# Keeping the sums of fc's weight blocks in DRAM: one transformer block with attention over a context, on one Trainium2 core

## The chip, the cores and the metric

The kernel runs on one core of a Trainium2 chip. Its time is the device time of one execution in microseconds; a measurement is the median of several executions, and shorter is better. The engines of the core have names in the profile: PE (TensorE, matrix products), DVE (VectorE), ACT (ScalarE), POOL (GpSimd) and SP (SyncE, which here only issues DMA transfers). The program gives each engine its own list of instructions, issued in the order in which the kernel's code calls them, and they wait for each other by semaphores.

## The reference, cut to what matters

Everything is float32. There are B = 4 batches; a batch has L = 512 rows of D = 512 numbers, and the hidden layer of the MLP has 2048 columns.

```python
def layer_norm(x, w, b): ...
x   = layer_norm(hidden_states, ln1_w, ln1_b)
q   = x @ q_w + q_b                       # 16 heads of 32
k   = encoder_hidden_states @ k_w + k_b
v   = encoder_hidden_states @ v_w + v_b
out = softmax(q @ k.T / sqrt(32), masked) @ v
hidden = out @ cproj_w + cproj_b + hidden_states
y   = layer_norm(hidden, ln2_w, ln2_b)
y   = gelu(y @ fc_w + fc_b)               # fc:   512 -> 2048
y   = y @ proj_w + proj_b                 # proj: 2048 -> 512
return hidden + y
```

## The kernel before

**Two parts.** The first part runs the attention of all batches as 32 blocks (16 groups of four heads, two halves each). The order is written out by hand: `put(p, ...)` names the other work that is filled into block p, and the program is issued in that order on every engine. Most of the MLP of batch 0 and half of that of batch 1 are such fillings. The second part, `last_mlps`, does the rest of batch 1's MLP (pairs 4 to 7 of fc and proj) and all of the MLPs of batches 2 and 3, one after the other.

**fc by seven products.** fc works on pairs of 128-column blocks of its weight; a batch has 8 pairs. `fc_seven` computes one pair by Winograd's form of Strassen's method: weight and input are cut into 2 by 2 blocks, and seven block products replace eight. Each of the seven is two matmuls, which stand as four rows in the trace (L518), so a pair is 28 rows. The products want sums of blocks: of the input (`y_sums`, once a batch, written to `ys` and into `yT`), and of the weight pair (`a_sums`, four subtractions or additions of 128 x 256 numbers: s1, s2, s3 and s4). These and all other sums stand in the trace at L472 (`add`) and L469 (`sub`). The products come in the order a11, a12, s2, s3, s1, s4, a22; the fourth takes the input sum t3 (written into `yT`), the seventh t4 (in `ys`). DVE then adds the products together into `ga` (or `gt`), and ACT applies gelu (L539).

**Where the weight sums are made.** For batch 0 and the first four pairs of batch 1, `fc_sums` makes them on POOL into `wsum` (s3 overwrites a block of the raw weight). In the second part `load_wa(c)` (L598, SP queue) loads the raw pair c into one of two buffers inside the tile `gt`, and `sum_wa(c)` makes its sums on DVE. `fc_pair(c)` issues `sum_wa(c + 1)` on DVE ahead of the additions of its own pair c.

**proj by seven products, some split once more.** `project` multiplies the gelu output `ga` (cut into g11, g12, g21, g22) with proj's weight (b11 to b22) by the same seven products, q1 to q7. `g_sums` (two pairs at a time) and `p_sums` make the sums. A plain product is 16 matmuls, 32 rows at L701 or L719. In batches 2 and 3 the products 3, 6, 7 and 5 are cut once more by `forty_nine`, which makes seven small products of four 128-wide matmuls (56 rows at L664); in batch 3 product 2 is, too. Each such split wants `x_sums` of its left side (three operations on DVE and one on POOL) and `w_sums` of its right side (four on DVE, from the list `to_split`, taken off by `split(n)`).

**Other work around it.** POOL copies a part of each attention block's transposed probabilities (`pT`, L335) while SP moves the rest by DMA (L340); the `av` products (L357) of block p are issued two blocks later and wait for both. `load_hid` loads the rows of a batch to which proj's result is added (SP, L413) and adds proj's bias on POOL (`add_row`, L368); for batch 2 it stands after pair 5 of batch 1. `load_xn` (L406), the loads of proj's weight (L461, L817) and the stores (L714, L786) share the SP queue. `stat2` (L127) computes layer-norm statistics on DVE.

Of the kernel before, what the change touches and what calls it, by code (L numbers as in the profile page):

```python
# [12 lines left out]
F32 = mybir.dt.float32  # L13
# [37 lines left out]
def xattn_block(ctx: ExitStack, tc: tile.TileContext, x, encT, mask, q_w, k_w, v_w, c_w, fc_w, p_w, vecs, rows, out):  # L51
# [422 lines left out]
    def a_sums(a11, a12, a21, a22, s1, s2, s3, s4, engine=None):  # L474
        add(engine or nc.vector, s1, a21, a22)
        sub(s3, a11, a21, engine)
        sub(s2, s1, a11, engine)
        sub(s4, a12, s2, engine)
# [18 lines left out]
    def acc_half(name):  # L497
        return acc_tile(name).rearrange("p (i l) -> p i l", i=2)
# [7 lines left out]
    def fc_seven(b, c, g, a, s, half, q=None):  # L506
# [35 lines left out]
        if q is None:  # L542
            gelus()

    fc_pairs = [(0, c) for c in range(NP)] + [(SPLIT, c) for c in range(FIRST * FQ // 2)]

    def raw_pair(b, c):
# [2 lines left out]
    def fc_sums():  # L550

        while count[3] < len(fc_pairs) and count[3] < count[4] + 2:
            b, c = fc_pairs[count[3]]
            if ("fcw", b, 2 * c + 1) not in S:
                return
            x, y = raw_pair(b, c)
            s = wsum[:, count[3] % 2]
            a_sums(x[:, :2], x[:, 2:], y[:, :2], y[:, 2:], s[:, 0], s[:, 1], y[:, :2], s[:, 2], nc.gpsimd)
            S["ws", b, c] = s[:, 0], s[:, 1], y[:, :2], s[:, 2]
            count[3] += 1  # L560

# [32 lines left out]
    ws = [gt[:, i * 2048 + 1024 : i * 2048 + 2048].rearrange("p (i k f) -> p i k f", i=4, k=2) for i in range(2)]  # L594

    def load_wa(c):
        for i in range(2):
            nc.sync.dma_start(out=wa[c % 2][:, i], in_=fc_w[:, 2 * c + i, :, :])  # L598

    def sum_wa(c):  # L600
        a = wa[c % 2]
        a_sums(a[:, 0, :2], a[:, 0, 2:], a[:, 1, :2], a[:, 1, 2:], *(ws[c % 2][:, i] for i in range(4)))

    def p_sums(c):

# [4 lines left out]
    def last_mlps():  # L610
# [73 lines left out]
            a11, a12, a21, a22 = (ga[:, c, k, j * HL : (j + 1) * HL] for j in range(2) for k in range(2))  # L684
            a_sums(a11, a12, a21, a22, gs[:, 0, c], gs[:, 1, c], a21, gs[:, 2, c])

        def fc_pair(b, c, sums):
            sums()
            fc_seven(b, c, ga[:, c], [wa[c % 2][:, i] for i in range(2)],
                     [ws[c % 2][:, i] for i in range(4)], half_tile)  # L690

        def project(b, pairs, sums, turns, middle):
            g11, g12, g21, g22 = (ga[:, :, k, j * HL : (j + 1) * HL] for j in range(2) for k in range(2))
            b11, b12, b21, b22 = (pb[:, :, k, j * HL : (j + 1) * HL] for k in range(2) for j in range(2))
            t1, t2, t3, t4 = pt[:, 0], pt[:, 1], b12, pt[:, 2]
            s1, s2, s3, s4 = gs[:, 0], gs[:, 1], g21, gs[:, 2]

            def product(o, a, w, ts_=range(2)):
                for t in ts_:
                    for c in pairs:  # L700
                        nc.tensor.matmul(  # L701
                            o[:, t], a[:, c, ts(t, P)], w[:, c], start=(c == pairs[0]), stop=(c == pairs[-1])
                        )

            def hid(i, j, t):
                return S["hid", b, 2 * i + t][:, j * HL : (j + 1) * HL]

            def join(engine, i, j, src):
                for t in range(2):
                    add(engine, hid(i, j, t), src[:, t], hid(i, j, t))  # L710

            def store(i, j):
                for t in range(2):
                    nc.sync.dma_start(out=out[b, ts(2 * i + t, P), j * HL : (j + 1) * HL], in_=hid(i, j, t))  # L714

            q1 = acc_half(f"q1p_{b}")
            steps = [(t, c) for c_ in (pairs[:-1], pairs[-1:]) for t in range(2) for c in c_]
            for n, (t, c) in enumerate(steps):
                nc.tensor.matmul(  # L719
                    q1[:, t], g11[:, c, ts(t, P)], b11[:, c],  # L720
                    start=n == 0, stop=c == pairs[-1], skip_group_check=t > 0,
                )
            nc.scalar.copy(p1p, q1)
            sums()
            if b > SPLIT:
                if b == B - 1:
                    x_sums(g12, x_more)
                else:
                    split(4)
                x_sums(s4, g11)  # L730
                if b == B - 1:
                    forty_nine(b, "2", u3p, g12, b21, x_more, 4)
                    q2 = u3p
                else:
                    q2 = acc_half(f"q2p_{b}")
                    product(q2, g12, b21)
                turns()
                join(nc.gpsimd, 0, 0, p1p)
                join(nc.gpsimd if b == B - 1 else nc.vector, 0, 0, q2)
                store(0, 0)  # L740
                x_sums(s2, g12)
                if b < B - 1:
                    split(4)
                forty_nine(b, "3", u3p, s4, b22, g11, 0)
                join(nc.gpsimd, 0, 1, u3p)
                x_sums(s3, s4)
                forty_nine(b, "6", u2p, s2, t2, g12, 1)
                add(nc.vector, u2p, u2p, p1p)
                x_sums(s1, s2)
                forty_nine(b, "7", u3p, s3, t3, s4, 2)  # L750
                add(nc.vector, u3p, u3p, u2p)
                for i, j, src in ((0, 1, u2p), (1, 0, u3p), (1, 1, u3p)):
                    join(nc.gpsimd, i, j, src)
                forty_nine(b, "5", p1p, s1, t1, s2, 3)
                join(nc.vector, 0, 1, p1p)
                join(nc.vector, 1, 1, p1p)
            else:
                q2 = acc_half(f"q2p_{b}")
# [12 lines left out]
                product(q7, s3, t3)  # L771
                add(nc.vector, u3p, q7, u2p)
                for i, j, src in ((0, 1, u2p), (1, 0, u3p), (1, 1, u3p)):
                    join(nc.gpsimd, i, j, src)
                q5 = half_tile(f"q5p_{b}")
                product(q5, s1, t1)
                join(nc.vector, 0, 1, q5)
                join(nc.vector, 1, 1, q5)
            store(0, 1)
            store(1, 1)  # L780
            middle()
            q4 = half_tile(f"q4p_{b}"), acc_half(f"q4p_{b}")
            for t in range(2):
                product(q4[t], g22, t4, (t,))
                add(nc.vector, hid(1, 0, t), q4[t][:, t], hid(1, 0, t))
                nc.sync.dma_start(out=out[b, ts(2 + t, P), :HL], in_=hid(1, 0, t))  # L786

        half = FIRST * FQ // 2
        to_split = (
            w_sums(2, pb[:, :, 0, HL:]) + w_sums(3, pt[:, 0])  # L790
            + w_sums(0, pb[:, :, 1, HL:]) + w_sums(1, pt[:, 1]) + w_sums(4, pb[:, :, 1, :HL])
        )
        splits = {(B - 2, 1): 2, (B - 2, 3): 3, (B - 2, 5): 3, (B - 1, 1): 2, (B - 1, 3): 2}

        def split(n):
            for _ in range(n):
                to_split.pop(0)()

        for b, pairs, new in (
            (SPLIT, range(half, NP), range(half)), (SPLIT + 1, range(NP), ()), (SPLIT + 2, range(NP), ())  # L800
        ):
            for c in pairs:

                def sums(b=b, c=c):
                    if c + 1 < NP:
                        sum_wa(c + 1)
                    split(splits.get((b, c), 0))

                fc_pair(b, c, sums)
                if c + 2 < NP:  # L810
                    load_wa(c + 2)
                elif b + 1 < B:
                    load_wa(c + 2 - NP)
                if new:
                    n = (c - half + 2) % half
# [2 lines left out]
                if c % 2 == 0 and c != pairs[0]:  # L818
                    g_sums(c - 2)

                if (b, c) in ((SPLIT, half + 1), (B - 1, half - 1)):
                    load_hid(max(b, SPLIT + 1), range(NT))
                if b == B - 3 and c < NP - 1:
                    stat2(B - 1, c - pairs[0])
                if b == B - 2:
# [7 lines left out]
            def sums(b=b, new=new):  # L833
                for c in new[::2]:
                    p_sums(c)

            def turns(b=b):
                if b + 1 < B:
# [4 lines left out]
            def middle(b=b):  # L843
                if b + 1 < B:
                    y_sums(b + 1)
                    sum_wa(0)

            project(b, pairs, sums, turns, middle)

# [120 lines left out]
    def put(p, *work, before=()):  # L970

        work = [item for part in work for item in part]
        ahead[p] = list(before)
        fills[p] = work
# [18 lines left out]
    put(9, c[:1], do(lambda: attend(3, 1)), x2[:2], c[1:2], x2[2:], stat(0, 0), c[2:3], stat(0, 1),  # L993
        c[3:], stat(0, 2), x3, stat(0, 3), rs(0))
    k, q, v = A(8)
    put(10, [k], norm(0, 0, 1), [v], norm(0, 2, 3), do(fc_sums), [q], t2, do(lambda: y_sums(0)))
    k, q, v = A(9)
    put(11, [k, v], some(2), pb_(0))

    x1, x2, x3, x4 = inputs(3)  # L1000
    put(12, [q], some(2), x1)
# [53 lines left out]
    run(mlp + norm(2, 2, 3))  # L1055
    p_sums(first_c)
    load_wa(first_c + 1)
    sum_wa(first_c)
    c = C(B - 1)
    run(c[:2])  # L1060
    p_sums(first_c + 2)
# [47 lines left out]
```

## Time and profile before

| what | value |
|---|---|
| median of 3 runs | 771.92 us (770.52 to 774.0) |
| the profiled execution | 771.6 us |
| its span, first to last instruction | 769.8 us |
| granted TensorE clock in it | 1.000 |
| PE busy | 762.7 us (99%) |
| DVE busy | 616.4 us (80%) |
| ACT busy | 336.8 us (44%) |
| POOL busy | 298.1 us (39%) |
| DMA moved | 119.37 MB, 155 GB/s on average |

The span is 1.8 us shorter than the execution's time: that much lies before its first and after its last instruction. Rows of the timeline give a start, a duration, the engine, the line of the kernel, the operation, what it writes and reads, how many instructions were merged, and in brackets how long the engine had been idle before and who released it. Rows of the chain give a start, a duration, the engine and the line: it is the sequence of work that ended last, followed back from the end. A pair of fc in the second part is 28 rows of L518; batch 1 has its pairs 4 to 7 from about 523 us on, batch 2 its eight pairs from about 577 us, batch 3 from about 673 us.

### The profile page before, as it was taken

Reading aid. Unit: us, or ns where it says so; the run is one execution under the profiler, and the core shown is the slowest. Engines: PE = TensorE matmul, PEld = TensorE weight load, DVE = VectorE, ACT = ScalarE, POOL = GpSimd, SP = SyncE. Lnnn points to the kernel's source line nnn. Section 1 sums busy time; section 2 is a strip of 40 time slices with the busy share of each in tenths; the row PEclk is TensorE's granted clock in tenths of the full one; section 3 lists DMA queues with packets and bytes.
Section 4 is the critical chain, followed back from the end, with each engine's and each line's share of the span. In section 5 each row is a group of like instructions: output and inputs, shape, how many; then the busy total and the mean of one; then the engine's idle time right before and its main releaser. Section 6 shows DMA issues by size and latency. Waiting matters only on the chain.

```text
span 769.8 us, 12991 instructions
## 1 busy us (share of the span) xinstructions
PE 762.7 (99%) x4450; PEld 519.1 (67%) x4450; DVE 616.4 (80%) x1263; ACT 336.8 (44%) x760; POOL 298.1 (39%) x311
## 2 busy tenths in 40 slices
PE   9999999999999999999999999999899999999998
PEld 6656555566654745565554566447788889988897
DVE  3889899887899757877887989776858997679872
ACT  2676766564775454638753567401102221022200
POOL 1525447378454363235565544330320004202052
PEclk9999999999999999999999999999999999999999
DMA  8978689466766666565756777773523310024001
GB/s 327 319 224 225 179 208 259 101 158 180 215 173 161 182 188 169 139 184 136 176 134 179 206 223 180 171 241 129 172 96 85 93 55 14 31 85 147 0 16 41
DMA packets 54817, 119.37 MB, mean 155 GB/s; under 512 B 10416, under 2 KB 13616, under 8 KB 54624
## 3 DMA queue, kind: packets, MB, share of 16 engines
q1 hardware_dynamic: 53712, 115.71, 54.1%
q0 software_dynamic: 896, 2.82, 1.2%
q8 instruction: 35, 0.57, 0.3%
q14 instruction: 30, 0.25, 0.1%
q10 hardware_dynamic: 144, 0.02, 0.0%
HBM read 58.22 MB, written 6.82 MB: 84 GB/s over the span
## 4 chain that ended last, share of the span: by engine, by line
PE 97%; DVE 2%; DMA 0%; issue 0%; ACT 0%; POOL 0%; DVEq 0%; POOLq 0%
PE q L518 24%; PE accp L574 11%; PE sc L260 8%; PE av L357 8%; PE accv L240 8%; PE acck L217 7%; PE accq L229 7%; PE r L664 7%; PE accc L397 7%; PE q4p L701 2%; PE q1p L719 2%; PE tp L158 2%; PE q2p L701 1%; DVE ga L472 1%; PE warm L901 1%; PE q3p L701 0%
## 5 line engine op out<-in xcount | busy, mean ns | idle before, releaser
L270 ACT ACTIVATE ptt<-ptt,mn 128x512 f32<-128x512 f32 x256 | 181.6, 711 | 149.8 <-DVE mn L266 149.8
L266 DVE CUSTOM_DVE_ANT_0 ptt<-sc,mb 128x512 f32<-128x512 f32 x256 | 160.5, 682 | 18.7 <-PE sc L260 18.6
L278 DVE STREAM_TRANSPOSE tb<-ptt 128x1024 f32<-128x1024 f32 x128 | 153.5, 1218 | 0.3 <-ACT ptt L270 0.2
L335 POOL COPY pT<-tb 32x1088 f32<-32x1088 f32 x96 | 104.5, 1088 | 39.9 <-DVE oT L362 14.6
L574 PE MATMUL accp<-pbt,gt 128*128 128x512 f32 x192 | 84.9, 596 | 0.0
L518 PE MATMUL q<-yT,gt 128*128 128x256 f32 x320 | 78.9, 379 | 0.0
L539 ACT ACTIVATE ga<-ga,vec 128x512 f32<-128x512 f32 x40 | 26.7, 714 | 98.5 <-DVE ga L472 98.5
L574 PEld LDWEIGHTS accp<-pbt,gt 128*128 128x128 f32 x192 | 35.8, 190 | 45.9 <-issue 39.4
L518 PEld LDWEIGHTS q<-yT,gt 128*128 128x128 f32 x320 | 60.8, 190 | 8.7 <-issue 0.5
L260 PE MATMUL sc<-pbt 32*128 32x512 f32 x512 | 65.3, 614 | 0.0
L240 PEld LDWEIGHTS accv<-ptt,xe 128*128 128x128 f32 x512 | 59.1, 192 | 7.4 <-DVE mn L266 4.7
L518 PE MATMUL q<-ys,gt 128*128 128x256 f32 x240 | 61.7, 379 | 0.0
L240 PE MATMUL accv<-ptt,xe 128*128 128x128 f32 x512 | 60.0, 276 | 0.0
L217 PE MATMUL acck<-xe,ptt 128*128 128x512 f32 x128 | 59.1, 604 | 0.0
L229 PE MATMUL accq<-xe,ptt 128*128 128x512 f32 (+1 forms) x136 | 58.3, 573 | 0.0
L397 PE MATMUL accc<-wc,oT 128*128 128x512 f32 x128 | 56.4, 596 | 0.0
L518 PEld LDWEIGHTS q<-ys,gt 128*128 128x128 f32 x240 | 45.5, 190 | 6.6 <-DVE gt L469 0.4
L270 ACT ACTIVATION_READ_ACCUMULATOR ptt<-ptt,mn 128x1 f32 x256 | 47.8, 187 | 0.0
L252 POOL TENSOR_TENSOR v<-v,row 128x512 f32<-128x512 f32 x16 | 20.5, 1282 | 67.6 <-ACT v L245 67.4
L357 PE MATMUL av<-pT,v 128*32 128x256 f32 x768 | 46.4, 382 | 0.0
L229 PEld LDWEIGHTS accq<-xe,ptt 128*128 128x128 f32 x136 | 25.0, 190 | 30.8 <-issue 23.2
L397 PEld LDWEIGHTS accc<-wc,oT 128*128 128x128 f32 x128 | 23.8, 190 | 30.8 <-issue 27.4
(182 smaller groups left out, 1186.3 us busy)
## 6 DMA issues: line engine op xcount, KB each, us to landing
pT<-tb SPq DMA_DIRECT2D x288, 136.0 KB, 2.4
pbt<-p_w_dram SPq DMA_DIRECT2D x40, 256.0 KB, 3.1
gt<-fc_w_dram SPq DMA_DIRECT2D x40, 256.0 KB, 2.7
gt<-tb SPq DMA_DIRECT2D x48, 136.0 KB, 2.4
xe<-tb SPq DMA_DIRECT2D x48, 136.0 KB, 2.4
pbt<-fc_w_dram SPq DMA_DIRECT2D x24, 256.0 KB, 3.7
ptt<-k_w_dram SPq DMA_DIRECT2D x16, 256.0 KB, 3.6
xe<-encT_dram SPq DMA_DIRECT2D x16, 256.0 KB, 5.0
```

Source lines behind the costliest of these rows:

```text
L217: nc.tensor.matmul(acc, S["wk", w][:, d, :], eT[:, d, :], start=(d == 0), stop=(d == ND - 1))
L229: nc.tensor.matmul(acc, S["wq", w][:, d, :], xT[:, d, c], start=(d == 0), stop=(d == ND - 1))
L240: nc.tensor.matmul(acc[:, ts(t, P)], eT[:, d, ts(t, P)], S["wv", w][:, d, :], start=(d == 0), stop=(d == ND - 1),)
L260: nc.tensor.matmul(S["sc", w, qt][h], qT[r, ts(qt, P)], kT[r, :], start=True, stop=True)
L266: nc.vector.tensor_tensor_reduce(out=s, in0=S["sc", w, qt][h], in1=S["mb", w // NG], scale=1.0, scalar=FMAX, op0=ALU.add, op1=ALU.min, acc ...
L270: nc.scalar.activation(s, s, AF.Exp, bias=mn, scale=-1.0, accum_out=S["sums", w][:, qt, h : h + 1])
L278: nc.vector.transpose(tv[:, qt % 2, 2 * k : 2 * k + 2], S["ps", w, qt, k])
L335: nc.gpsimd.tensor_copy(pT[ts(i, HD), i], tb[ts(i, HD), i])
L357: nc.tensor.matmul(av[ts(h, HD), : 2 * P].rearrange(shape, **kw), v[:, t, ts(h, HD)], p[t][h], start=(t == 0), stop=(t == NT - 1),)
L397: nc.tensor.matmul(acc, S["oT", b][:, g, ts(t, P)], wc[:, g, :], start=(g == 0), stop=(g == NG - 1))
L518: nc.tensor.matmul(o, x[:, k], y[:, k], start=(k == 0), stop=(k == 1))
L574: nc.tensor.matmul(acc, gT[q % 2][:, k, ts(t, P)], S["pw", b, q * FQ + k], start=(k == 0), stop=(k == FQ - 1))
```

## The change

For batch 0, `fc_sums` sends the four sums of each weight pair to a DRAM tile, `sums_dram`, by two POOL DMAs behind the sums (128 x 768 and 128 x 256 numbers). In the second part `sum_wa` is gone: `load_wa(c)` issues three transfers on SP, the first raw block (256 KB), the used half of the second (128 KB) and all four sums (512 KB).

Product 2 of batch 2's proj is cut once more by `forty_nine`, as batch 3's already was; the two now share that code. Its `x_more` lies in the two buffers of the loaded sums, so the loads of pairs 0 and 1 of batch 3 stand behind it, inside `project`. The weight splits of `to_split` are taken in another order, all of them in batch 2: two ahead of each of its pairs 0 to 6, two and four in its proj.

`load_hid` of batch 2 (four loads on SP and four additions on POOL) moves from behind pair 5 of batch 1 into batch 1's `project`, behind `p_sums`. `y_sums(0)`, two operations on DVE and two on POOL, moves from the end of block 10's fillings to behind the k product of block 11; on POOL it now stands behind block 10's four `pT` copies, on DVE behind the softmax operations of block 11.

```diff
+    sums_dram = dram.tile([NP, P, 4, 2, P], F32, tag="ws", name="ws")
...
             a_sums(x[:, :2], x[:, 2:], y[:, :2], y[:, 2:], s[:, 0], s[:, 1], y[:, :2], s[:, 2], nc.gpsimd)
+            if b == 0:
+                nc.gpsimd.dma_start(out=sums_dram[c, :, :3], in_=s)
+                nc.gpsimd.dma_start(out=sums_dram[c, :, 3], in_=y[:, :2])
...
     def load_wa(c):
-        for i in range(2):
-            nc.sync.dma_start(out=wa[c % 2][:, i], in_=fc_w[:, 2 * c + i, :, :])
-
-    def sum_wa(c):
-        a = wa[c % 2]
-        a_sums(a[:, 0, :2], a[:, 0, 2:], a[:, 1, :2], a[:, 1, 2:], *(ws[c % 2][:, i] for i in range(4)))
+        nc.sync.dma_start(out=wa[c % 2][:, 0], in_=fc_w[:, 2 * c, :, :])
+        nc.sync.dma_start(out=wa[c % 2][:, 1, 2:], in_=fc_w[:, 2 * c + 1, 2:, :])
+        nc.sync.dma_start(out=ws[c % 2], in_=sums_dram[c])
...
-        def fc_pair(b, c, sums):
-            sums()
+        def fc_pair(b, c):
             fc_seven(b, c, ga[:, c], [wa[c % 2][:, i] for i in range(2)],
-                     [ws[c % 2][:, i] for i in range(4)], half_tile)
+                     [ws[c % 2][:, i] for i in (0, 1, 3, 2)], half_tile)
...
             if b > SPLIT:
-                if b == B - 1:
-                    x_sums(g12, x_more)
-                else:
-                    split(4)
+                x_sums(g12, x_more)
                 x_sums(s4, g11)
-                if b == B - 1:
-                    forty_nine(b, "2", u3p, g12, b21, x_more, 4)
-                    q2 = u3p
-                else:
-                    q2 = acc_half(f"q2p_{b}")
-                    product(q2, g12, b21)
+                forty_nine(b, "2", u3p, g12, b21, x_more, 4)
+                if b < B - 1:
+                    load_wa(0)
+                    load_wa(1)
                 turns()
                 join(nc.gpsimd, 0, 0, p1p)
-                join(nc.gpsimd if b == B - 1 else nc.vector, 0, 0, q2)
+                join(nc.gpsimd, 0, 0, u3p)
                 store(0, 0)
                 x_sums(s2, g12)
-                if b < B - 1:
-                    split(4)
                 forty_nine(b, "3", u3p, s4, b22, g11, 0)
                 join(nc.gpsimd, 0, 1, u3p)
+                split(2)
                 x_sums(s3, s4)
                 forty_nine(b, "6", u2p, s2, t2, g12, 1)
                 add(nc.vector, u2p, u2p, p1p)
                 x_sums(s1, s2)
+                split(4)
...
         to_split = (
-            w_sums(2, pb[:, :, 0, HL:]) + w_sums(3, pt[:, 0])
-            + w_sums(0, pb[:, :, 1, HL:]) + w_sums(1, pt[:, 1]) + w_sums(4, pb[:, :, 1, :HL])
+            w_sums(4, pb[:, :, 1, :HL]) + w_sums(0, pb[:, :, 1, HL:]) + w_sums(1, pt[:, 1])
+            + w_sums(2, pb[:, :, 0, HL:]) + w_sums(3, pt[:, 0])
         )
-        splits = {(B - 2, 1): 2, (B - 2, 3): 3, (B - 2, 5): 3, (B - 1, 1): 2, (B - 1, 3): 2}
...
             for c in pairs:
-
-                def sums(b=b, c=c):
-                    if c + 1 < NP:
-                        sum_wa(c + 1)
-                    split(splits.get((b, c), 0))
-
-                fc_pair(b, c, sums)
+                split(2 if b == B - 2 and c < NP - 1 else 0)
+                fc_pair(b, c)
                 if c + 2 < NP:
                     load_wa(c + 2)
-                elif b + 1 < B:
+                elif b == SPLIT:
                     load_wa(c + 2 - NP)
...
-                if (b, c) in ((SPLIT, half + 1), (B - 1, half - 1)):
-                    load_hid(max(b, SPLIT + 1), range(NT))
+                if (b, c) == (B - 1, half - 1):
+                    load_hid(b, range(NT))
...
             def sums(b=b, new=new):
                 for c in new[::2]:
                     p_sums(c)
+                if new:
+                    load_hid(b + 1, range(NT))
...
             def middle(b=b):
                 if b + 1 < B:
                     y_sums(b + 1)
-                    sum_wa(0)
...
-    put(10, [k], norm(0, 0, 1), [v], norm(0, 2, 3), do(fc_sums), [q], t2, do(lambda: y_sums(0)))
+    put(10, [k], norm(0, 0, 1), [v], norm(0, 2, 3), do(fc_sums), [q], t2)
...
-    put(11, [k, v], some(2), pb_(0))
+    put(11, [k], do(lambda: y_sums(0)), [v], some(2), pb_(0))
...
     load_wa(first_c + 1)
-    sum_wa(first_c)
```

More of the change, by code (lines that the diff above doesn't have):

```diff
@@ L789, in last_mlps @@
         to_split = (
-            w_sums(2, pb[:, :, 0, HL:]) + w_sums(3, pt[:, 0])
-            + w_sums(0, pb[:, :, 1, HL:]) + w_sums(1, pt[:, 1]) + w_sums(4, pb[:, :, 1, :HL])
+            w_sums(4, pb[:, :, 1, :HL]) + w_sums(0, pb[:, :, 1, HL:]) + w_sums(1, pt[:, 1])
+            + w_sums(2, pb[:, :, 0, HL:]) + w_sums(3, pt[:, 0])
         )
-        splits = {(B - 2, 1): 2, (B - 2, 3): 3, (B - 2, 5): 3, (B - 1, 1): 2, (B - 1, 3): 2}
         def split(n):
-            for _ in range(n):
+            for _ in range(min(n, len(to_split))):
                 to_split.pop(0)()
```

## The prediction

> **What bounds the kernel now.** I read the shares of the engines and the chain that ended last, then who waited for whom on PE, then the chain piece by piece.
>
> ```profile
> span 769.8 us, 12991 instructions
> PE 762.7 (99%) x4450; PEld 519.1 (67%) x4450; DVE 616.4 (80%) x1263; ACT 336.8 (44%) x760; POOL 298.1 (39%) x311
> PE 97%; DVE 2%; DMA 0%; issue 0%; ACT 0%; POOL 0%; DVEq 0%; POOLq 0%
> ...
> PE q1p L719 <- ACT ga L539: 2.6, 1, 2.6
> ```
>
> PE is the bound, busy 762.7 of 769.8 us. Taking work off DVE is therefore worth only the PE time that DVE costs today, and after the start the list of PE's waits holds one entry: 2.6 us before `q1p`. A gain can come from there, from stretches in which PE ran its rows slower than elsewhere, and from fewer rows. The chain has the pieces:
>
> ```profile
> 163.34 2.55 PE sc L260 x16
> 181.00 1.93 PE sc L260 x16
> 535.75 2.65 DMA gt<-fc_w_dram
> 543.71 1.64 DVE ga L469
> 545.36 1.68 DVE gs L469
> 547.06 1.64 DVE gs L469
> 552.20 0.73 ACT ga L539
> ...
> 576.79 1.73 PE q L518 x8
> 578.52 46.89 PE q L518 x216
> 632.31 6.91 PE q2p L701 x32
> 641.18 25.09 PE r L664 x224
> 673.18 48.35 PE q L518 x224
> 728.44 31.26 PE r L664 x280
> ```
>
> Between 535.75 and 552.97 the chain leaves PE for DMA, DVE and ACT; in the rest of the second part PE follows PE. A row of fc takes 48.35 / 224 = 0.216 us, a pair 28 of them, 6.04. Batch 3's proj, with five split products, runs 280 rows in 31.26 us, 0.112 each, which is the rate of batch 2's four (25.09 / 224).
>
> **1. The wait before q1p.** It closes batch 1's fc. The timeline shows why DVE was late:
>
> ```profile
> 538.42 0.42 DVE L472 TENSOR_TENSOR gt<-gt 128x256 f32<-128x256 f32 x1 [1.12 <-DMA gt<-fc_w_dram]
> 541.86 6.29 POOL L368 TENSOR_TENSOR hl<-hl,row 128x512 f32<-128x512 f32 x4 [30.95 <-PE q L518]
> 542.55 1.13 DVE L472 TENSOR_TENSOR gs<-ga 128x512 f32<-128x512 f32 x1
> 547.64 2.75 PE L719 MATMUL q1p<-pbt,ga 128*128 128x256 f32 x12
> 548.62 0.68 DVE L127 BATCH_NORM_STATS2 st<-pbt 128x6 f32<-128x512 f32 x1
> 550.22 1.95 DVE L472 TENSOR_TENSOR ga<-q,ga 128x512 f32<-128x512 f32 x3
> 553.94 3.62 PE L701 MATMUL q2p<-pbt,ga 128*128 128x256 f32 x16
> 554.29 0.69 DVE L469 TENSOR_TENSOR ga<-ga 128x512 f32<-128x512 f32 x1
> ```
>
> DVE first waits for the raw pair to land (1.12 us), with the additions of pair 6 queued behind. Then `g_sums` meets POOL's four `hl` additions (1.57 us each): its four operations cost 1.13 + 1.64 + 1.68 + 1.64 = 6.1 us, where one without POOL beside it takes 0.69, four 2.8. The change takes both away: no weight sum is left in DVE's queue, and `load_hid` moves. DVE then has per pair 0.69 + 1.95 us of additions, some 0.9 of statistics and, every second pair, 2.8 of `g_sums`: 4.9 on average against 6.04. PE ends pair 7 at 547.64, its last product reaches DVE some 0.3 later, the last addition ends at 548.6 and the first gelu (0.73) at 549.5. PE meanwhile has the 12 rows that need nothing of pair 7, until 547.64 + 12 x 0.216 = 550.2. All 16 take 3.46, so `q2p` starts at 551.10 instead of 553.94: **-2.84 us**. The bounds are 0 (DVE late for another reason) and -2.84 (more there is not).
>
> The Trainium skill, "SBUF — State Buffer", section "Who interferes with whom", states that a DVE operation with two SBUF inputs and a GpSimd operation that reads SBUF exclude each other, the second waiting until the first has finished. The 1.64 us beside POOL's additions against 0.69 agree with it.
>
> What `load_hid` meets next: in `project`, POOL's four additions fall on the eight DVE operations of `p_sums`, which also wait for the last proj weights. Four of them stretched cost 4 x 0.95 = 3.8 us. Behind them on DVE stand the `yT` turns, the join of q2 and the sum of q6, and ahead of that sum DVE sat idle:
>
> ```profile
> 566.53 0.69 DVE L472 TENSOR_TENSOR u2p<-q6p,p1p 128x512 f32<-128x512 f32 x1 [3.06 <-PE q6p L701]
> 628.32 1.33 ACT L539 ACTIVATE ga<-ga,vec 128x512 f32<-128x512 f32 x2 [3.71 <-DVE ga L472]
> ```
>
> That 3.06 (the first row), the 2.8 by which DVE comes earlier, which PE's earlier q6 takes back, and the later idle time before q7's sum cover nearly all; no matmul of this batch reads `p_sums`, and u2p itself is wanted one product (3.45 us) later. SP issues these loads ahead of `load_xn`, which waits for PE's transposes anyway, and of the stores, for which nobody waits. Cost 0; uncovered, 3.8 us.
>
> **2. One product split.** 32 rows in 6.91 us become 56 at 0.112, 6.27: **-0.64 us**. Are its sums there in time? PE ended batch 2's fc at 625.4, but the last gelus ran until 629.65 (the second row above), since DVE lagged. With DVE on time they end near 627.6, `g_sums` at 630.4, and s2 of `x_sums(g12)` two operations later, 631.8; the third small product wants it at 632.31 + 2 x 8 x 0.112 = 634.1. The rest of DVE's new work here (five additions and three sums, less two splits and the join of q2) is what batch 3 carried at the same 0.112. Between none and 1 us of stall I take none, because batch 3's row is the same code. Uncovered it is the 3 x 0.69 us of the sums.
>
> **3. A stretch in batch 2's fc.** Its 224 rows took 1.73 + 46.89 = 48.62 us, batch 3's 48.35. The first weight sums stood on DVE there: **-0.27**. The 14 splits that this fc now carries (0.69 each, 9.7 us) replace 28 weight sums of 0.42 and eight earlier splits (17.3 us), so DVE ends lighter; before, a heavier DVE cost PE no more than the 0.27.
>
> **4. The loads.** A pair brings 896 KB instead of 512 in 6.04 us, 148 GB/s. The first block's buffer comes free early; the other transfers (640 KB) go out when PE ends pair c, with two SP issues some 0.9 us into pair c + 1, and s2 of pair c + 2 is wanted 8 rows into it: 6.04 + 1.73 - 0.9 = 6.9 us later.
>
> ```profile
> gt<-fc_w_dram SPq DMA_DIRECT2D x40, 256.0 KB, 2.7
> hl<-xa SPq DMA_DIRECT2D x4, 256.0 KB, 5.2
> wc<-c_w_dram SPq DMA_DIRECT2D x1, 1024.0 KB, 9.0
> ```
>
> The ends are 2.7 us for one block and 9.0 for a megabyte at the crowded start. Four blocks issued in a row in this stage landed in 5.2, nearest to 640 KB in two transfers; I take 4 to 5, below 6.9: cost 0. In batch 1, 512 KB of proj weights queue behind on SP and land later, for `p_sums` alone; the four `hl` loads have left that place.
>
> The Trainium skill, "DMA: Bandwidth & Descriptors", section "Anatomy of one DMA", gives about 2.0 us plus bytes over 436e3 for a DMA of the GpSimd path; an estimate from that page for 640 KB is 3.5 us, and by it the cost is 0 too.
>
> **5. POOL in batch 0.** Sixteen DMA issues are added, and `y_sums(0)` moves.
>
> ```profile
> L400 POOL DMA_DIRECT2D xa<-h x6: 539/542/639, 278.5 to 414.5; - x6
> 160.47 0.73 POOL L472 TENSOR_TENSOR wsum<-pbt 128x256 f32<-128x256 f32 x1
> 162.09 1.16 DVE L469 TENSOR_TENSOR ys<-yT 128x512 f32<-128x512 f32 x1
> 167.24 1.28 POOL L469 TENSOR_TENSOR yT<-yT 128x512 f32<-128x512 f32 x1
> 171.17 0.68 DVE L266 CUSTOM_DVE_ANT_0 ptt<-sc,mb 128x512 f32<-128x512 f32 x1
> 174.66 1.03 PE L518 MATMUL q<-ys,wsum 128*128 128x256 f32 x4
> 185.41 4.47 POOL L335 COPY pT<-tb 32x1088 f32<-32x1088 f32 x4
> 192.61 1.86 PE av L357 x32
> ```
>
> An issue held POOL for 0.54 us, say 0.57 with its wait. After pairs 2 to 7 that puts 1.1 us before the next `pT` copies, and POOL is idle in 61% of the span: cost 0. The tight place is the first fc pair. The two `ys` operations (from 162.09) no longer stand before the `oT` that frees a buffer for the scores, which took 2.55 us instead of 1.93: **-0.62**. On POOL the eight sums need 6.0 (8 x 0.75), four issues 2.3, the copies 4.5, `yT` 1.28: it is ready at 160.47 + 14.1 = 174.5. PE wants it for the fourth product at 174.66 + 0.86 - 0.62 = 174.9. On DVE the `ys` operations start behind the last softmax operation, at 171.85, among POOL's copies; between 0.69 each and 0.69 plus a whole copy (4.47 / 4 = 1.1) they end at 173.2 to 175.4, and PE wants t2 at 174.66 - 0.62 = 174.04. So 0 to 1.4 us is given back; at the 1.16 us that such an operation took beside POOL's sums (162.09) they end at 174.17, so I take **+0.2**. The copies that ended at 189.9 end near 191; their `av` starts at 192.61 - 0.6: covered.
>
> **Sum.** -2.84 - 0.64 - 0.27 - 0.62 + 0.2 = -4.2 us. The profiled execution took 771.6 (its span and 1.8 around it), 0.3 below the median 771.92 of the runs shown: 771.6 - 4.2 = **767.4 us**.
>
> **The rivals.**
> *POOL and DVE at the first pair.* Both `ys` operations wait for a whole copy: t2 comes at 175.4, 1.4 us late, and POOL's second `ys` operation and the copies behind slip as much, so that the next `av` waits some 0.2. With 1.6 in place of 0.2: 768.8. For it: 1.64 against 0.69 above. Against: no row shows a copy of 32 partitions beside such an operation. That full wait is the rule of the Trainium skill's "SBUF — State Buffer", "Who interferes with whom".
> *The wait stays.* DVE is late at pair 7 all the same, for instance because `g_sums` and the statistics (3.7 us) stand directly before its additions. Without the 2.84: 770.2. Against: by the count above DVE has 0.7 us in hand there.
> *Slower: the sums land late.* At the 9.0 us of the megabyte's row each of the 14 pairs whose loads go out inside the loops waits 2.1: +29, 797. At 7.8 it is 14 x 0.9 = 12.6: 780. It decides from 7.5 us, where 8.4 takes 767.4 to 775.8. Against: 5.2 us for a megabyte in this stage.
>
> **How the numbers follow.** Forecast 0.56, its own range 766.3 to 768.6; first rival 0.20; the wait stays 0.13; slower 0.11. A change of 0.5% (3.9 us: below 768.06, or above 775.78) is about what a measurement of this kernel can tell from none. The forecast lies 0.7 us beyond it, and the runs before spread from 770.52 to 774.0: of its 0.56 I give 0.44 to faster, of the first rival's 0.04; of the slower one's 0.10 to slower. Faster has 0.48; the rest, 0.42, is within 0.5%. The range, 765.8 to 771.8, ends above the wait that stays and leaves out the late loads and a little at each end.
>
> **What would show it.** Right: no wait for ACT at `q1p` in batch 1, and `q2p` 3.5 us behind its start; 280 rows of L664's kind in batch 2 at 0.112; 48.35 us for fc in both batches; the scores before the first fc pair back at 1.93. Wrong: PE waits for the loaded sums in fc; POOL's issues hold it for their landing time and not 0.54; DVE sits before proj weights until q6's sum is late; the first fc pair loses more than 1.4 us.

## The result and the profile after

The changed kernel takes 768.77 us (median of nine runs, 768.15 to 769.1); the kernel before took 772.51 in nine runs too (770.52 to 774.8). The ratio of the means, 768.63 and 772.75, is 0.9947, with a 95% interval of 0.9933 to 0.9961: faster by 0.5%, the size that the prediction took as about the least that can be told from none; the interval excludes no change. The forecast was 767.4 us. The profiled execution took 768.29 (its span and 1.8 around it), against 771.6 before.

From the page and from the list of PE's waits of the changed kernel:

```profile
span 766.5 us, 13025 instructions
PE 760.6 (99%) x4474; PEld 520.1 (68%) x4474; DVE 594.7 (78%) x1188; ACT 337.1 (44%) x761; POOL 312.6 (41%) x330
PE 98%; DVE 1%; POOL 0%; ACT 0%; issue 0%; POOLq 0%
...
PE q L518 <- POOL yT L469: 1.1, 1, 1.1
```

PE is still the bound. DVE lost 21.7 us of work, POOL gained 14.5, and PE lost 2.1. The wait of 2.6 us before `q1p` is gone, and a new one of 1.1 has come: a product of fc (L518) waits for POOL's `yT`. The chain shows where in the run each step fell. First some pieces of the kernel before that the prediction did not show (start, duration, engine, line):

```profile
161.48 1.86 PE av L357 x32
179.14 1.86 PE av L357 x32
523.63 12.10 PE q L518 x56
554.10 3.45 PE q2p L701 x16
625.40 6.91 PE q1p L719 x32
639.22 1.96 PE tp L158 x16
```

and the same places of the changed kernel (its `r` is at L665):

```profile
161.27 1.86 PE av L357 x32
...
179.65 1.86 PE av L357 x32
...
524.15 24.17 PE q L518 x112
548.33 3.45 PE q1p L719 x16
551.78 3.45 PE q2p L701 x16
...
574.46 48.35 PE q L518 x224
622.81 6.91 PE q1p L719 x32
629.72 6.25 PE r L665 x56
635.97 1.75 PE tp L158 x16
637.71 25.01 PE r L665 x224
662.73 6.91 PE q4p L701 x32
```

The differences of the distances give each stretch its own cost, free of where the run stood when it reached it:

| stretch | before | after | difference | predicted |
|---|---|---|---|---|
| first fc pair, `av` to `av` | 17.66 | 18.38 | +0.72 | -0.42 |
| batch 1, fc's start to `q2p` | 30.47 | 27.63 | -2.84 | -2.84 |
| batch 2, fc | 48.61 | 48.35 | -0.26 | -0.27 |
| batch 2, product 2 | 6.91 | 6.25 | -0.66 | -0.64 |
| batch 2, transposes and four split products | 27.05 | 26.76 | -0.29 | 0 |

The sum is -3.33, and the two profiled executions are 3.3 us apart (their starts and ends differ by -0.2 and +0.25, which nearly cancel). The means of the nine runs are 4.1 apart; the run with `y_sums(0)` alone moved, below, shows where the rest may come from. One row is off in sign. The timeline of the first fc pair in the changed kernel (start, duration, engine, line, operation; in brackets the idle time before and who ended it) has its parts:

```profile
163.61 0.64 POOL L561 DMA_DIRECT2D ws<-wsum  x1 [0.30 <-POOL wsum L469]
168.16 0.56 POOL L561 DMA_DIRECT2D ws<-wsum  x1 [0.30 <-POOL wsum L469]
169.25 5.27 POOL L335 COPY pT<-tb 32x1088 f32<-32x1088 f32 x4
174.61 1.27 POOL L469 TENSOR_TENSOR yT<-yT 128x512 f32<-128x512 f32 x1
...
163.06 2.00 PE L260 MATMUL sc<-pbt 32*128 32x512 f32 x16
173.83 1.03 PE L518 MATMUL q<-ys,wsum 128*128 128x256 f32 x4
175.93 1.13 PE L518 MATMUL q<-yT,pbt 128*128 128x256 f32 x4 [1.07 <-POOL yT L469]
...
171.38 0.69 DVE L469 TENSOR_TENSOR ys<-yT 128x512 f32<-128x512 f32 x1
172.10 1.46 DVE L469 TENSOR_TENSOR ys<-yT,ys 128x512 f32<-128x512 f32 x1
```

The scores are back at 2.00 in this view, as predicted: a row of 2.00 here is a piece of 1.93 where the chain stays on PE. DVE's second sum, which the third product takes, is ready at 173.56, ahead of the 173.83 at which that product starts. But POOL's `yT` ends at 175.88, and the fourth product would have been free to start at 174.69, the 0.86 behind the third that the prediction counted between products. The idle time shown is 1.07. What it costs is 18.38 - 17.04 = 1.34, where 17.04 is the same distance with no wait in it (it is measured below): matmuls that follow at once also overlap the end of the one ahead by 0.17 (1.03 long, 0.86 apart), which is lost with a wait, and the four behind the wait stand as 1.13 instead of 1.03. The same holds for the wait before: shown as 2.6, worth 2.84.

The loads of the sums in the list of DMA issues (KB each, median us from issue to landing):

```profile
gt<-ws SPq DMA_DIRECT2D x20, 512.0 KB, 3.4
```

The sums land 3.4 us after their issue, below the estimated 4 to 5 and well below the 6.9 of the window.

### The profile page after: what moved, and what is told of

The parts are those of the page before. It is cut to its first block, busy times and chain, and to the rows that moved or that the text cites. A ratio compares the mean times of both kernels' runs of the same rounds, so it can differ in the third digit from the quotient of the medians.

```text
span 766.5 us, 13025 instructions
## 1 busy us (share of the span) xinstructions
PE 760.6 (99%) x4474; PEld 520.1 (68%) x4474; DVE 594.7 (78%) x1188; ACT 337.1 (44%) x761; POOL 312.6 (41%) x330
## 4 chain that ended last, share of the span: by engine, by line
PE 98%; DVE 1%; POOL 0%; ACT 0%; issue 0%; POOLq 0%
PE q L518 25%; PE accp L578 11%; PE r L665 8%; PE sc L260 8%; PE av L357 8%; PE accq L229 7%; PE accc L397 7%; PE accv L240 7%; PE acck L217 7%; PE q4p L701 2%; PE q1p L719 2%; PE tp L158 2%; PE warm L891 1%; DVE ptt L266 0%; PE q3p L701 0%; PE q5p L701 0%
## 5 line engine op out<-in xcount | busy, mean ns | idle before, releaser
L518 PE MATMUL q<-yT,gt 128*128 128x256 f32 x320 | 78.9, 380 | 0.0
L518 PEld LDWEIGHTS q<-yT,gt 128*128 128x128 f32 x320 | 60.9, 190 | 8.6 <-DMA xa<-pbt 0.2
L518 PE MATMUL q<-ys,gt 128*128 128x256 f32 x240 | 61.6, 380 | 0.0
L472 DVE TENSOR_TENSOR ga<-q,ga 128x512 f32<-128x512 f32 (+1 forms) x60 | 36.2, 603 | 21.4 <-PE q L518 19.4
L518 PEld LDWEIGHTS q<-ys,gt 128*128 128x128 f32 x240 | 45.7, 190 | 6.1
```

Of the source, the lines that this page charges most:

```text
L518: nc.tensor.matmul(o, x[:, k], y[:, k], start=(k == 0), stop=(k == 1))
```

## Experiments

Runs of the kernel before scattered from 770.6 to 775.4 us across these experiments, so each kernel is compared by its ratio to the runs of before made beside it, and by distances within its trace. Two things move a run. One is its start: the `av` ahead of the first fc pair stands at 160.7 to 163.1 us in these traces, and this is no part of any comparison by distances. The other is the granted clock: of 42 executions of the kernel before, 20 had a mean of 1.000 and took 770.6 to 773.7 us, and 22 had 0.998 (one 0.996) and took 773.1 to 775.4. So a ratio to before also holds how many of its runs had the lower clock, and the distances decide.

### Which of the two causes made the wait before q1p

The prediction named two: the weight sums in DVE's queue, and POOL's additions of `load_hid` beside `g_sums`. Two kernels each remove one. The first is the kernel before with `load_hid` alone moved:

```diff
-                if (b, c) in ((SPLIT, half + 1), (B - 1, half - 1)):
-                    load_hid(max(b, SPLIT + 1), range(NT))
+                if (b, c) == (B - 1, half - 1):
+                    load_hid(b, range(NT))
...
                     p_sums(c)
+                if new:
+                    load_hid(b + 1, range(NT))
```

> The kernel before with one part of the change: load_hid of batch 2 moved into batch 1's proj. The prediction named two causes of the 2.6 us wait before q1p, the weight sums in DVE's queue and POOL's additions beside g_sums. If both are needed for it, moving load_hid alone leaves about half, 1 to 1.5 us, and the time falls by 1.3 to 1.8 us. Rival: POOL's additions alone make DVE late (g_sums 6.1 us instead of 2.8, more than the 2.84 lost), so the wait goes entirely with the weight sums still on DVE: q2p starts 3.46 us behind q1p, and the time falls by 2.84 us, 0.37%.

It took 768.99 us, ratio 0.995 (0.9933 to 0.9968), which is more than the 0.37% expected of 2.84 us; the clock that the next section reads accounts for a part. Its chain, and DVE at the end of batch 1's fc in its timeline:

```profile
548.02 3.45 PE q1p L719 x16
551.48 3.45 PE q2p L701 x16
...
574.16 1.73 PE q L518 x8
575.90 46.89 PE q L518 x216
```

```profile
543.61 0.69 DVE L469 TENSOR_TENSOR ga<-ga 128x512 f32<-128x512 f32 x1
```

All 16 matmuls of `q1p` run in one piece of 3.45 us: the wait is wholly gone, with all weight sums still on DVE, as the rival said. DVE's own wait for the raw pair is still there (1.08 us in this trace) and costs PE nothing. The stretch in batch 2's fc (1.73 + 46.89) is still there, as it should be if the weight sums cause that one.

The second is the changed kernel with `load_hid` put back:

```diff
-                if (b, c) == (B - 1, half - 1):
-                    load_hid(b, range(NT))
+                if (b, c) in ((SPLIT, half + 1), (B - 1, half - 1)):
+                    load_hid(max(b, SPLIT + 1), range(NT))
...
-                if new:
-                    load_hid(b + 1, range(NT))
```

> The changed kernel with load_hid of batch 2 back behind pair 5 of batch 1, the rest as changed. If the weight sums that left DVE give part of the gain, at most half of the wait returns: 0 to 1.4 us above the changed kernel. Rival (POOL's additions alone): g_sums takes about 6 us again, the last addition of pair 7 ends some 3.3 us later, and the wait for ACT at q1p comes back whole, 2.6 us or so; about 2.8 us above the changed kernel's 768.3 profiled time, and hardly below the kernel before plus 0.64 and 0.27 of gains.

It took 770.87 us, ratio 0.9977 (0.9967 to 0.9986). From its list of waits and its timeline:

```profile
PE q1p L719 <- ACT ga L539: 2.0, 1, 2.0
```

```profile
543.83 6.81 POOL L368 TENSOR_TENSOR hl<-hl,row 128x512 f32<-128x512 f32 x4 [32.05 <-PE q L518]
544.51 1.65 DVE L469 TENSOR_TENSOR ga<-ga 128x512 f32<-128x512 f32 x1
546.08 1.75 DVE L469 TENSOR_TENSOR gs<-gs,ga 128x512 f32<-128x512 f32 x1
547.87 1.64 DVE L469 TENSOR_TENSOR gs<-ga,gs 128x512 f32<-128x512 f32 x1
```

Without a single weight sum on DVE, 2.0 of the 2.6 us are back, between the two answers expected and nearer to the rival's. By the distance from fc's start to `q2p` (29.89 us) it is 2.26 of 2.84. The three stretched sums took 3.0 us longer than three of 0.69; less the 0.7 that the prediction counted in hand, this is the 2.3. The four loads of `load_hid` moved with the additions, but no DVE row here waits for a DMA. So the additions on POOL beside `g_sums` make the wait by themselves; the weight sums add some 0.6 to it and make none without them. The Trainium skill, "SBUF — State Buffer", section "Who interferes with whom", gives the rule behind it: a DVE operation with two SBUF inputs and a GpSimd operation that reads SBUF exclude each other for a whole instruction. The 1.64 to 1.75 us here against 0.69 in the run above agree with it.

### The first fc pair

The `ys` sums at their new place, in the kernel before and nothing else:

```diff
-    put(10, [k], norm(0, 0, 1), [v], norm(0, 2, 3), do(fc_sums), [q], t2, do(lambda: y_sums(0)))
+    put(10, [k], norm(0, 0, 1), [v], norm(0, 2, 3), do(fc_sums), [q], t2)
...
-    put(11, [k, v], some(2), pb_(0))
+    put(11, [k], do(lambda: y_sums(0)), [v], some(2), pb_(0))
```

> The kernel before with y_sums(0) moved behind the k product of block 11, and nothing else. If the 1.07 us that PE waits for POOL's yT in the changed kernel come from the place alone, PE waits about as long here. Rival: the place costs nothing while POOL has no stores to issue; the copies start about 2.9 us earlier (four issues at 0.56 and two waits of 0.3), yT is ready near 173.5, PE does not wait, and the scores before take 1.93 instead of 2.55 us: 0.6 us faster than the kernel before up to the first fc pair.

One run, 773.15 us, with a late start (its first `av` here stands 0.5 us behind that of before). Its chain:

```profile
162.01 1.86 PE av L357 x32
...
179.05 1.86 PE av L357 x32
...
552.80 1.39 PE q1p L719 x4
554.19 4.88 PE q2p L701 x16
```

From `av` to `av` 17.04 us, 0.62 less than before, and PE waits nowhere in it: the predicted -0.62 is exact, and the move alone is all gain. POOL's copies here take 4.47 us and its `yT` stands idle 1.53 us for DVE, so POOL has time in hand as long as no store is put in front.

This kernel keeps the wait before `q1p`, and its last two lines show a second price of it. The wait is 2.48 us, and behind it the granted clock is 0.50 for 3.4 us (from about 553.5 to 556.9 us; 1.00 on either side): the last four matmuls of `q1p` take 1.39 us instead of 1.13, and `q2p` 4.88 instead of 3.45, 1.69 us in all. In the profiled execution of the kernel before, the wait of 2.58 us left the clock at 1.00. A stretch of this length makes a mean clock of 0.998, which 21 of the 42 executions of before had, and one had 0.996; where in those it fell was not recorded. None of the 35 executions of the kernels without that wait was below 0.999, and none of the 20 of the two kernels whose traces show a wait of 1.8 or 2.0 us. An estimate from this: half the executions of before lose a further 1.7 us to the wait, 0.9 on average; with the 3.3 of the two traces this is 4.2, near the 4.1 between the means.

The changed kernel with `y_sums(0)` back at its old place is the opposite edit.

> The changed kernel with y_sums(0) back at the end of block 10's fillings. POOL then makes yT ahead of the copies, near 171, so PE's wait of 1.07 us goes; DVE's two operations stand before oT again and the scores stretch to about 2.55 us. Net 0.4 to 0.5 us below the changed kernel if the stores delay nothing else; if the copies that follow (2.6 us later than in the kernel before) now make the next av wait, no gain or a loss of up to 2 us.

One run, 769.6 us, again with a late start. The distance is 180.76 - 163.08 = 17.68 us with the scores at 2.56 and no wait for `yT`: the 0.62 is not won, and the stores cost nothing in this pair (17.66 before). That is 0.70 below the changed kernel, where 0.4 to 0.5 was expected; the next block takes 0.1 us longer than the 13.47 it takes before. So the 1.34 needs both edits: the stores stand ahead of `yT` only when `y_sums(0)` stands behind them.

Next, both edits kept, but the stores of the first two pairs on POOL behind `y_sums(0)`:

```diff
...
             if b == 0:
-                nc.gpsimd.dma_start(out=sums_dram[c, :, :3], in_=s)
-                nc.gpsimd.dma_start(out=sums_dram[c, :, 3], in_=y[:, :2])
+                stores.append((c, s, y))
+                if c > 1:
+                    store_sums()
...
-    put(11, [k], do(lambda: y_sums(0)), [v], some(2), pb_(0))
+    put(11, [k], do(lambda: (y_sums(0), store_sums())), [v], some(2), pb_(0))
```

Here `store_sums` issues the same two DMAs for every pair in the list.

> The changed kernel with the stores of the first two pairs' sums issued on POOL behind y_sums(0) instead of ahead of block 10's copies. If PE's wait of 1.07 us for yT came from the four issues (0.54 to 0.64 us each and two waits of 0.3) ahead of the copies, the copies start about 2.8 us earlier, end before DVE's two ys operations begin, yT is ready near 173.5 and PE does not wait: 1.1 to 1.3 us below the changed kernel, a ratio of about 0.993 to the kernel before. Rival: the place of y_sums is what costs, and PE still waits 0.5 us or more; or the stores delay the sums of pair 2 and the next copies, and an av waits instead.

It took 768.24 us, ratio 0.9943 (0.9929 to 0.9957). The first pair takes 17.05 us, with no wait for `yT`. Then the next `av` waits, by the timeline:

```profile
188.32 4.47 POOL L335 COPY pT<-tb 32x1088 f32<-32x1088 f32 x4
...
192.84 1.93 PE L357 MATMUL av<-pT,v 128*32 128x256 f32 x32 [0.71 <-DMA ptt<-q_w_dram]
```

The list of waits names a DMA there, but that load, issued at 190.06, had not landed in full when `av` began (3.3 us to landing), and the last `pT` transfer, issued at 189.36, had landed 1 us before (2.4 us). The copies of `pT`, which `av` reads, end at 192.79, just ahead of it. So four issues in a row push POOL's copies behind PE, and half of the 1.34 is lost again one block on: the last rival. The next run takes the issues away from POOL: the same kernel with these four stores on SP's queue (`store_sums(nc.sync)` there, POOL for the later pairs).

> The changed kernel with the stores of the first two pairs' sums issued on the SP queue, behind y_sums(0); the other six pairs as changed. POOL then has its order of work as without stores up to pair 2: yT is ready near 173, PE does not wait for it, and POOL's next copies end near 191, ahead of the av that wants them. From the av ahead of the first fc pair to the next but one 30.5 us instead of 31.85 in the changed kernel: 1.3 us faster than it, span near 765.2, ratio about 0.993, faster than both kernels. Rival: SP is held by these stores long enough to delay other loads, and PE waits for a DMA instead.

It took 767.03 us (766.23 to 767.69), ratio 0.992 (0.9901 to 0.9938). Its chain:

```profile
160.87 1.86 PE av L357 x32
...
177.91 1.86 PE av L357 x32
...
191.38 1.86 PE av L357 x32
```

The first pair takes 17.04 us and the next block 13.47, both without a wait: it was the issues on POOL, and with `y_sums(0)` at its new place POOL has room for them at neither of the two places tried. A wait of 0.5 us is left at a later `av` (222.36 us), behind the twelve `pT` issues on SP; its cause was not tried. This version beats both kernels: its slowest run, 767.69, is below the fastest of the changed kernel, 768.15, and from the `av` ahead of the first fc pair to the last addition it takes 601.05 us against 601.83.

### The split and the loaded sums

The changed kernel with product 2 of batch 2 plain:

```diff
-                x_sums(g12, x_more)
+                if b == B - 1:
+                    x_sums(g12, x_more)
                 x_sums(s4, g11)
-                forty_nine(b, "2", u3p, g12, b21, x_more, 4)
+                if b == B - 1:
+                    forty_nine(b, "2", u3p, g12, b21, x_more, 4)
+                    q2 = u3p
+                else:
+                    q2 = acc_half(f"q2p_{b}")
+                    product(q2, g12, b21)
...
```

The four weight splits that this product no longer needs go back into batch 3's fc, and its result is joined on DVE again, as before.

> The changed kernel with product 2 of batch 2's proj plain again (32 rows), its x_sums gone and the right side's four splits back in batch 3's fc. By the prediction's second term these 32 rows take 6.91 us instead of 56 rows in 6.25 us: from the start of batch 2's q1p to the start of its q4p 0.66 us more, and nothing else moves. Rival: DVE's new work in that proj costs something that the plain product gives back, so the stretch is the same or shorter.

One run, 769.13 us. Its chain:

```profile
629.59 6.91 PE q2p L701 x32
636.49 1.96 PE tp L158 x16
638.45 25.10 PE r L665 x224
```

From q1p's start (622.68) to q4p (663.55) it takes 40.87 us, against 39.92 in the changed kernel: the split is worth 0.95, of which 0.66 is the product, 0.21 the transposes behind it and 0.09 the products after them. The prediction had the first alone.

All of the change but the DRAM: weight sums on DVE as before (`y_sums(0)` at its old place), with `load_hid` moved, product 2 split and the weight splits where the change puts them.

```diff
...
-        nc.sync.dma_start(out=ws[c % 2], in_=sums_dram[c])
...
+    def sum_wa(c):
+        a = wa[c % 2]
+        a_sums(a[:, 0, :2], a[:, 0, 2:], a[:, 1, :2], a[:, 1, 2:], *(ws[c % 2][:, i] for i in range(4)))
...
+                if c + 1 < NP:
+                    sum_wa(c + 1)
                 split(2 if b == B - 2 and c < NP - 1 else 0)
```

> All of the change except its first part: the weight sums are made on DVE again (no stores on POOL, no loads of sums), y_sums(0) stands at its old place, but load_hid is moved, product 2 of batch 2 is split and the splits stand in batch 2. If the loads of the sums are what makes room for the split, DVE has per pair of batch 2 2.64 us of additions, 1.7 of weight sums, 1.4 of g_sums and 1.4 of splits, 7.1 against PE's 6.04: it falls some 7 us behind over the batch, PE waits for it in fc or at q1p, and the kernel is 3 to 6 us slower than the changed one. Rival: the backlog is taken up by the 6.9 us of q1p and by buffers, PE loses less than 1 us, and the first part of the change was worth next to nothing by itself: 767.5 to 769 us.

It took 770.77 us, ratio 0.9978 (0.9967 to 0.9989). From its list of waits:

```profile
PE r L664 <- DVE gt L469: 1.8, 1, 1.8
```

The split product waits 1.8 us for its sums of the left side. From fc's start in batch 2 to q4p this kernel takes 91.30 us, the kernel with `load_hid` alone moved 89.49, the changed kernel 88.27. With the weight sums on DVE the split loses 1.8; without them it wins 0.95. So, with the weight splits placed as the change has them, the sums in DRAM are what pays for the split; another placing of the splits with the weight sums on DVE was not tried. The whole is 2.0 us above the changed kernel where 3 to 6 was expected: PE waited at the split product alone, not in fc or at `q1p`, and the first fc pair has no stores (17.67 us).

The changed kernel with a further DRAM copy of 512 KB on SP ahead of each load of sums:

```diff
+        nc.sync.dma_start(out=more_dram[c], in_=sums_dram[c])
         nc.sync.dma_start(out=ws[c % 2], in_=sums_dram[c])
```

> The changed kernel with one transfer added per pair of the second part: the pair's 512 KB of sums are copied from DRAM to DRAM on the same queue, ahead of the load of the sums, so that this load is issued later and lands beside more traffic. By the prediction's fourth term the sums have 6.9 us to land and took 3.4 in the changed kernel: they land later, at 4.5 to 6 us, PE waits for none of the 14 pairs inside the loops, and the second part's fc stretches stay at 24.17, 48.35 and 48.35 us. Rival (the loads are near their limit): from landing 7 us on each pair waits, 5 us or more in all.

One run, 767.83 us. From its DMA issues and its chain:

```profile
gt<-ws SPq DMA_DIRECT2D x20, 512.0 KB, 5.5
```

```profile
523.62 24.42 PE q L518 x112
574.18 48.35 PE q L518 x224
```

The sums land 2.1 us later, and batch 1's fc loses 0.25 us, which was not expected and which the list of waits does not name; batch 2's and batch 3's fc lose nothing (48.35 each). In batches 2 and 3 the loads have some 2 us in hand, as the estimate of 4 to 5 against 6.9 said.

### The moves without the sums

The kernel before with both moves (`load_hid` and `y_sums(0)`) and nothing else; its edits are the first and the third diff above.

> The kernel before with the two moves alone: load_hid of batch 2 into batch 1's proj and y_sums(0) behind the k product of block 11. No sums in DRAM, no further split. If the sums in DRAM and the split are worth what their stores cost at the first fc pair (1.22 us from batch 2's fc to its q4p against 1.34 before), this kernel is as fast as the changed one: span near 766.6 us, ratio about 0.9945. Rival: the named change carries part of the gain, and this kernel is 1 us or more slower than the changed one.

It took 767.65 us (767.5 to 768.65), ratio 0.9931 (0.9914 to 0.9947). That is not slower than the changed kernel (768.77); the ratio is the lower one in part because eight of the eleven runs of before beside it had the lower clock. From the `av` ahead of the first fc pair to the last addition it takes 601.71 us, the changed kernel 601.83. Two calls moved do what the whole change does, because what the sums in DRAM win in batch 2 (0.95 + 0.26 = 1.21) their stores take away at the first pair (1.34). The version with four stores on SP keeps both: from batch 1's fc to the last addition it takes 238.96 against 240.17 us here, and the difference is those 1.21. The 0.5 us at the later `av` is lost again.

## Why the prediction was right, and where it was not

The forecast of 767.4 lies 0.9 us below the profiled execution, 768.29. Two misses make this: the first fc pair cost 1.14 more than predicted (step 5), and 0.29 came behind the split that no step counted (step 2). That the second took back a part of the first was luck.

1. *The wait before q1p.* The size, -2.84, was exact, and so was the count that DVE has time in hand without the two causes. The share of the causes was wrong: the step said that the change "takes both away" as if both were needed. The weight sums had no cost of their own there. A call moved in the code gains the whole 2.84, as the run with `load_hid` alone shows. And 2.84 is the price in an execution whose clock stays at 1.00; the step did not count the 1.69 that the wait cost beyond it where the clock fell. So a part of the spread of before, 770.52 to 774.0, which the prediction took for noise, was probably this wait.

2. *One product split.* -0.66 against -0.64, and its sums were in time: the 56 rows of `r` stand in the chain as one piece. That its cover was the DVE time freed in fc was argued from batch 3's row; the run with weight sums on DVE shows it, with 1.8 us of wait where the uncovered price was put at 3 x 0.69 = 2.07. Left out were 0.29 us behind the split, of which 0.21 are the transposes (1.75 instead of 1.96).

3. *A stretch in batch 2's fc.* -0.26 against -0.27. It stayed in the three kernels that only move calls (48.61 to 48.62 us) and is gone in those without weight sums.

4. *The loads.* Cost 0, as predicted, with 3.4 us to landing. Of the eight `p_sums` operations that `load_hid` now meets, four were stretched, to 1.64 to 1.76 us; that was covered, but only just:

```profile
558.93 1.64 DVE L469 TENSOR_TENSOR ptt<-pbt,ptt 128x512 f32<-128x512 f32 x1
...
564.88 0.67 DVE L472 TENSOR_TENSOR u2p<-q6p,p1p 128x512 f32<-128x512 f32 x1
```

This timeline of the changed kernel has one of the four, and the sum that had 3.06 us of idle time ahead of it: now it has none, and PE still waits for nothing there.

5. *POOL in batch 0.* This is the step that failed, in its last term. The gain of 0.62 came. The +0.2 that was given back was 1.34: inside the bounds of 0 to 1.4, but the value was taken for the wrong operation. The prediction had PE waiting a little for t2 on DVE, which was in time, and `yT` on POOL ready at 174.5 for 174.9. It was ready at 175.88. From the first weight sum to there POOL took 15.6 us where 14.1 were counted: twice 0.30 of idle time before a store that reads what POOL itself has just written, 5.27 instead of 4.47 for the four copies, and 0.1 elsewhere. In the row it used, four of the six issues wait for DVE and none behind a write of POOL's own, so that row could not show the 0.30; and beside the copies of the row it used DVE ran no sums. And 0.4 us in hand behind a row of 17 instructions was too little to leave out of the sum.

The first rival put the place and the price right (1.6) and the mechanism only in part: one of the two `ys` operations was held, for 0.77 us, and the copies for 0.80, but it was `yT` behind the copies that was late. That its 768.8 is the median measured is luck: it has 0.26 too much at the first pair and, like the forecast, lacks the 0.29. *The wait stays* and *the sums land late* fell: no wait at `q1p`, and 2.1 us later landings cost 0.25 us in one of three fcs.

## What to carry to other kernels

Count time in hand on the queue that an added instruction stands in, not the engine's idle share: POOL was idle for 59% of the span, and 2.3 us of issues at one place still cost 1.34. When several causes lie behind one wait, take each away alone before paying for the larger edit; here a moved call was worth 2.84 us, and the new data path with its split 1.21, which its own stores took away. A wait that the list puts at 1.07 us cost 1.34, so price it by the distance between the same two pieces of the chain in the two kernels; and look at the granted clock behind a wait of PE in more than one execution, for one profile may show the cheap case.

## What the runs showed of the hardware

A store on POOL that follows POOL's own write starts 0.30 us after it, in all eight pairs of stores, and holds POOL for 0.56 to 0.64 us; the second of a pair follows at once and holds it for 0.54. Where the write was long past (the stores behind `y_sums(0)`), the 0.30 is gone. Copies of 32 partitions on POOL and DVE operations with two inputs of 128 partitions hold each other, as full tiles do: 4.47 became 5.23 to 5.27 us for four copies, and 0.69 became 1.46 for one of two subtractions, in all four traces in which they met. Behind a wait of PE of 2.48 us the granted clock was 0.50 for 3.4 us in one trace, and behind one of 2.58 us it stayed at 1.00 in another; what decides was not tried. In the second part the 16 transposes took 1.75 us behind 128-wide matmuls and 1.96 behind 256-wide ones; why was not tried. Where an instruction waits for several others, the one that the list names need not be the late one, as the `av` blamed on a weight load shows.
